# Closing layer 0's tile pools early, and reading the convolution's operands into their room

## The chip, the cores and the metric

The program runs on one core of one Trainium2 chip. Times are device microseconds (us) of one execution. The kernel before takes 4254.93 us, the median of three runs between 4251.25 and 4259.25.

## The reference, cut to what matters

Four layers work on x of shape 4 images x 128 channels x 64 x 64, seen as 128 x 4096 for an image.

```python
x = mamba2d(x)                    # layer 0: projections, a selective scan over 4096 positions, + x
x = x + L1(gn(x))                 # layer 1, see below
t = tokens(x)                     # from here on token-major
t = t + attn2(ln(t)); t = t + ffn(ln(t), L2)     # layer 2: linear attention, 64 experts
t = t + attn3(ln(t)); t = t + ffn(ln(t), L3)     # layer 3
# L1, the "convolution" over a hypergraph, with xf = tokens(gn(x)):
incidence = (dist(xf, xf) < 16)
vert = incidence @ (incidence.T @ (xf @ W_fc.T + b_fc) / deg_e) / deg_v
out = vert + xf
y = gamma * (out - mean(out, over all images)) * rsqrt(var + eps) + beta
return y * sigmoid(y)
```

The mean and variance of layer 1 run over all four images. So y can be made only when the last image's `vert` is done, and the hidden `out` of all images has to wait somewhere. Both `x1` (the output of layer 0) and `hg` (`out`) wait in DRAM, 2 MB an image each.

## The kernel before, in words

**Layers 0 and 1** are written in `layers01` as Python generators. `layer0` yields after each half state of the scan, `layer1(b)` after each piece of work on image b, and the driving loop interleaves layer 1 of image b with layer 0 of image b + 1. Image 3 of layer 1 has no layer 0 beside it and runs alone. Layer 1 of an image first reads the image's x1 in eight chunks `xn` (L457, queue of SyncE, one buffer for each chunk), normalises them on ScalarE (L458), and compares tokens panel by panel on TensorE (L499). At the end it makes `vert` chunk by chunk (L622, 64 matmuls a chunk); VectorE scales it into `rb` (L630), GpSimd adds xn (L631), and `rb` is written to `hg` (L635). When all images are done, five small operations make the scale and shift `bn` (L666 to L671).

**The end of layer 1**, `layer1_end`, takes sixteen units of 128 x 1024 elements. A unit reads `o` from hg (L683, issued on ScalarE's queue) and `x` from x1 (L685, on SyncE's queue), makes silu(o * scale + shift) on ScalarE (L686), adds it to x on GpSimd (L687), turns the sum into tokens by eight transposes on TensorE (L692), and copies the two PSUM tiles into `X`, one by ScalarE and one by VectorE (L694). The pool `l1e` has three buffers for each of o and x.

**Attention of layer 2**, `attn2`, first takes layernorm statistics of 16 blocks of 128 tokens on VectorE (L702), then makes z (L779, L781), turns it on TensorE (L782), and so on. It also reads its own weights (L740, L742) and the first experts' weights (`load`, L1020 and L1023).

**What sets the order.** The operations are written in program order, and a tile framework orders them on each engine by its own priorities; every engine and every DMA queue then runs its own list strictly in order. The tile pools lie in SBUF as a stack, on the left side unless `side="right"` is given; when a pool is closed, a later one takes its room. A pool without `reuse_waits="tile"` that takes room used before waits for all that was done in the pools there; with it, each tile waits for the tiles that it overlaps. DMA completions are counted on eight counters in turn, shared by all queues, and a DMA waits until the one before it on its counter has landed, so about eight are under way at most.

In the kernel before, the pools of layer 0, `l0p` and `l0bc`, stay open until the end of `layers01`, on the left. `X` and then `fe` (one group of experts' weights) are opened after that on the left, then `l1e`.

Of the kernel before, what the change touches and what calls it, by code (L numbers as in the profile page):

```python
# [7 lines left out]
F32 = mybir.dt.float32  # L8
F16 = mybir.dt.float16
FP8 = mybir.dt.float8e4  # L10
AF = mybir.ActivationFunctionType
ALU = mybir.AluOpType
AX = mybir.AxisListType
PSUM = bass.MemoryType.PSUM
DRAM = bass.MemoryType.DRAM

P = 128
B = 4
# [22 lines left out]
class Net:  # L41
# [33 lines left out]
    def layers01(self):  # L75
        nc, tc, a = self.nc, self.tc, self.a
# [9 lines left out]
        LAG = 6 * 2  # L86
        with ExitStack() as ctx:
            wp = ctx.enter_context(tc.tile_pool(name="aw", bufs=1))
            w2 = ctx.enter_context(tc.tile_pool(name="l0p", bufs=2))
            bcp = ctx.enter_context(tc.tile_pool(name="l0bc", bufs=5))  # L90
            tp = ctx.enter_context(tc.tile_pool(name="l1t", bufs=2))
            dp = ctx.enter_context(tc.tile_pool(name="l0d", bufs=3, space=DRAM))
            ip = ctx.enter_context(tc.tile_pool(name="l1i", bufs=1, space=DRAM))
# [2 lines left out]
            ps = ctx.enter_context(tc.tile_pool(name="aps", bufs=4, space=PSUM))  # L96
# [103 lines left out]
            def due(every=False):  # L200
                for w in list(waiting):
                    if every or w[0] <= self.tick:
                        waiting.remove(w)
                        w[1]()
# [445 lines left out]
            for b in range(B):  # L650
                l1 = layer1(b)
                if b < B - 1:
                    done = 0
                    for k in range(states):
                        next(l0, None)
                        self.tick += 1
                        due()
                        while done * states < work * (k + 1):
                            done += next(l1)
                for _ in l1:  # L660
                    self.tick += 1
                    due()
# [7 lines left out]
            nc.vector.tensor_tensor(bn[:, 1:2], bn[:, 2:3], bn[:, 0:1], ALU.mult)  # L670
            nc.vector.tensor_tensor(bn[:, 1:2], gb[:, 1:2], bn[:, 1:2], ALU.subtract)  # L671

    def layer1_end(self):

        nc = self.nc
        with self.tc.tile_pool(name="l1e", bufs=3) as tp, self.tc.tile_pool(
            name="l1eps", bufs=4, space=PSUM
        ) as ps:
            for b in range(B):
                for c in range(4):  # L680
                    sl = slice(c * 1024, (c + 1) * 1024)
                    o = tp.tile([P, 1024], F32, tag="o", name="o")
                    nc.scalar.dma_start(o, self.hg[b][:, sl])  # L683
                    x = tp.tile([P, 1024], F32, tag="x", name="x")
                    nc.sync.dma_start(x, self.x1[b][:, sl])  # L685
                    nc.scalar.activation(o, o, AF.Silu, scale=self.bn[:, 0:1], bias=self.bn[:, 1:2])  # L686
                    nc.gpsimd.tensor_tensor(x, x, o, ALU.add)  # L687
                    for h in range(2):
                        pt = ps.tile([P, 4, P], F32, tag="tr", name="ps_x")
                        for i in range(4):  # L690
                            k = 4 * h + i
                            nc.tensor.transpose(pt[:, i, :], x[:, k * P : (k + 1) * P], self.ident)  # L692
                        k = 8 * c + 4 * h
                        (nc.vector.tensor_copy if h else nc.scalar.copy)(self.X[:, b, k : k + 4, :], pt)  # L694


    def ln_stats(self, sp, b, j0, n, rs=None):
# [577 lines left out]
@with_exitstack  # L1275
def tile_kernel(ctx: ExitStack, tc: tile.TileContext, a, out):
    net = Net(tc, a)
    net.setup(ctx)
    net.layers01()
    xp = ctx.enter_context(tc.tile_pool(name="X", bufs=1))  # L1280
    net.X = xp.tile([P, B, NB, P], F32, tag="X", name="X")
    net.ew = ctx.enter_context(tc.tile_pool(name="fe", bufs=1))
    net.layer1_end()
    net.ahead = net.load(net.ew, "L2_ffn", 0)
    net.attn2()
    net.ffn("L2_ffn")
    net.ahead = net.load(net.ew, "L3_ffn", 0)
    net.attn3()
    net.ffn("L3_ffn", out)
# [48 lines left out]
```

## Time and profile before

| | |
|---|---|
| median of three runs | 4254.93 us |
| the profiled execution | 4245.77 us |
| its span (first to last instruction) | 4244.0 us |
| TensorE, busy | 3520.5 us, 83% of the span |
| VectorE, busy | 3014.7 us, 71% |
| GpSimd, busy | 2463.1 us, 58% |
| ScalarE, busy | 2088.3 us, 49% |
| last write of x1 issued (end of layer 0) | 2848.03 us from the span's start |
| first matmul of layer 1 on image 3 | 2882.45 us |
| last `hg` part computed, bn ready | 3324.5 us |
| last unit of `layer1_end` in X | 3388.8 us |
| first transpose of attention 2 | 3397.4 us |

Times "at" are counted from the start of the span. The busy shares are averages over stages with different limits: an engine at 83% overall can be idle for half of one stage.

### The profile page before, as it was taken

The page shows a single profiled execution, that of the slowest core. Times are in us where ns is not written, and L with a number is a line of the kernel's source. Part 1 is how long each engine was busy: PE and PEld are TensorE (multiplying, and loading weights), DVE is VectorE, ACT ScalarE, POOL GpSimd, SP SyncE. Part 2 cuts the span into 40 slices and gives each one's busy share as a digit, 9 for nine tenths or more (in the row PEclk, how much of TensorE's full clock was granted, in tenths as well). Part 3 has the DMA queues.
Part 4 walks back from the last instruction along what each step waited for, and adds up shares of the span by engine and source line. Part 5 has one row for each costly group of instructions (what it writes and reads, how often), then busy time and mean ns, then how long its engine had stood idle before and what let it go on. Part 6 is the DMA issues. An engine that isn't in the chain of part 4 may idle for free. (4 is left out here: it accounts for less than half of the span.)

```text
span 4244.0 us, 48880 instructions
## 1 busy us (share of the span) xinstructions
PE 3520.5 (83%) x17239; PEld 1963.5 (46%) x17239; DVE 3014.7 (71%) x4819; ACT 2088.3 (49%) x3547; POOL 2463.1 (58%) x1234
## 2 busy tenths in 40 slices
PE   6878858888897788888878888889999589788988
PEld 2333323444533334454334345435664378446844
DVE  5888879987666999866689997665420275746864
ACT  4556654455544545564454555521141287533841
POOL 5999889987786998867788887760000300001300
PEclk8989978999998889999988999999999699898999
DMA  3454534454364444545634454361113400053028
GB/s 105 152 147 146 156 109 134 138 137 138 108 187 139 127 132 137 153 117 146 184 107 135 125 150 126 110 222 70 65 63 112 158 1 1 1 198 124 1 80 299
DMA packets 261991, 523.94 MB, mean 123 GB/s; under 512 B 22346, under 2 KB 24562, under 8 KB 261746
## 3 DMA queue, kind: packets, MB, share of 16 engines
q1 hardware_dynamic: 250450, 501.45, 39.5%
q10 hardware_dynamic: 11296, 19.37, 1.4%
q8 instruction: 136, 2.23, 0.2%
q14 instruction: 109, 0.89, 0.1%
HBM read 443.15 MB, written 77.59 MB: 123 GB/s over the span
## 5 line engine op out<-in xcount | busy, mean ns | idle before, releaser
L286 POOL TENSOR_TENSOR db<-dx,bt 128x1024 f32<-128x1024 f32 x512 | 1203.0, 2353 | 329.3 <-DVE hs L304 214.2
L304 DVE TENSOR_TENSOR_SCAN hs<-hs,carry,db 128x512 f32<-128x512 f32 x812 | 1035.3, 1282 | 177.4 <-ACT hs L298 95.5
L298 ACT ACTIVATE hs<-dl,A 128x512 f32<-128x512 f32 x1024 | 706.5, 692 | 737.3 <-DVE ho L314 684.5
L499 PE MATMUL ps_g<-xn 128*128 128x512 f32 x1152 | 602.8, 654 | 100.7 <-DVE inc L502 74.8
L321 POOL TENSOR_TENSOR ho_s<-ho_s,ho 128x1024 f32<-128x1024 f32 x288 | 677.0, 2351 | 11.6 <-DVE ho L314 10.9
L314 DVE TENSOR_TENSOR ho<-hs,bt 128x1024 f32<-128x1024 f32 x464 | 563.3, 1214 | 1.6
L522 PE MATMUL ps_ed<-xs,inc 128*128 128x258 f16 x4096 | 507.9, 284 | 18.2 <-DVE inc L502 8.1
L522 PEld LDWEIGHTS <-inc 128*128 128x128 fp8e4 x4096 | 414.9, 102 | 131.9 <-issue 60.8
L502 DVE SCALAR_TENSOR_TENSOR inc<-ps_g,hcl,hb 128x512 fp8e4<-128x512 f32 x576 | 420.4, 736 | 35.3 <-PE ps_g L499 19.7
L499 PEld LDWEIGHTS ps_g<-xn 128*128 128x128 f32 x1152 | 216.2, 204 | 416.9 <-DVE inc L502 183.7
L342 PE MATMUL ps_y<-ho,cst 128*128 128x512 f32 x512 | 272.2, 674 | 110.5 <-POOL ho L310 93.1
L622 PE MATMUL ps_v<-inc_v,es 128*128 128x512 fp8e4 x1536 | 342.9, 382 | 19.4 <-DVE rb L630 9.4
L622 PEld LDWEIGHTS <-es 128*128 128x128 f16 x2048 | 202.6, 99 | 288.8 <-issue 63.6
L515 ACT CAST inc<-ps_t 128x512 fp8e4<-128x512 f32 x448 | 232.1, 600 | 96.2 <-PE ps_t L511 96.1
L903 POOL MEMSET G<- 128x128 f32 x2 | 0.4, 204 | 468.2 <-DMA b<-in_L_attn_bv 468.2
L224 PE MATMUL ps_c<-xt,wc 128*128 128x512 f32 x512 | 234.0, 611 | 12.5 <-DVE inc L502 6.8
L342 PEld LDWEIGHTS ps_y<-ho,cst 128*128 128x128 f32 x512 | 104.6, 214 | 269.7 <-POOL ho L310 123.8
L528 ACT COPY ed<-ps_ed 128x129 f32<-128x129 f32 x128 | 34.0, 266 | 377.6 <-PE ps_ed L522 377.6
L529 DVE TENSOR_TENSOR ed<-ps_ed,ed 128x129 f32<-128x129 f32 x128 | 36.6, 286 | 209.7 <-ACT ed L528 206.6
L304 DVE TENSOR_TENSOR_SCAN hs<-hs,db 128x512 f32<-128x512 f32 x116 | 141.3, 1223 | 53.8 <-POOL db L286 42.8
L538 POOL TENSOR_TENSOR ed<-ed,rdeg 128x512 f32<-128x512 f32 x32 | 33.3, 1040 | 250.1 <-DVE rdeg L534 250.1
L224 PEld LDWEIGHTS ps_c<-xt,wc 128*128 128x128 f32 x512 | 99.2, 197 | 139.0 <-issue 116.6
(302 smaller groups left out, 5599.9 us busy)
## 6 DMA issues: line engine op xcount, KB each, us to landing
bt<-bcd SPq DMA_DIRECT2D x512, 512.0 KB
inc<-inc SPq DMA_DIRECT2D x192, 256.0 KB
inc_v<-inc SPq DMA_DIRECT2D x96, 512.0 KB
w<-in_L_ffn_weight SPq DMA_DIRECT2D x32, 1024.0 KB
w2f<-in_L_ffn_weight SPq DMA_DIRECT2D x32, 1024.0 KB
strip<-inc SPq DMA_DIRECT2D x84, 256.0 KB
x<-x ACTq DMA_DIRECT2D x32, 256.0 KB
xn<-x SPq DMA_DIRECT2D x32, 256.0 KB
```

Source lines behind the costliest of these rows:

```text
L224: nc.tensor.matmul(s["ps"][h], wc[:, h, j, :], xt[:, j : j + T], start=j == 0, stop=j == 3)
L286: nc.gpsimd.tensor_tensor(db, s["dx"], bc(s["bt", n][:, 0, :], 2), ALU.mult)
L298: act(nc.scalar.activation(hs[:, k, :], s["dl"][:, k, :], AF.Exp, scale=A[:, k, n : n + 1]))
L304: nc.vector.tensor_tensor_scan(to[:, h, :], hs[:, h, :], db[:, h, :], init, ALU.mult, ALU.add)
L314: nc.vector.tensor_tensor(ho, hs, ct, ALU.mult)
L321: nc.gpsimd.tensor_tensor(s["sum", n // G], s["sum", n // G], ho, ALU.add)
L342: nc.tensor.matmul(s["y"][h], self.ident, t[:, h, :], start=False, stop=n == DS - 1 and k == len(terms) - 1,)
L499: nc.tensor.matmul(pq, xn[v // 4][:, v % 4 * P : (v % 4 + 1) * P], xn[c], start=True, stop=True)
L502: nc.vector.scalar_tensor_tensor(inc[:, v, :], pq, hc[:, v : v + 1], hb, ALU.subtract, ALU.is_gt, saturate=False)
L515: later(1, lambda: act(nc.scalar.copy(inc[:, v, :], pt, saturate=False)))
L522: nc.tensor.matmul(pe[:, : 2 * P + 2], inc[:, v, i * P : (i + 1) * P], xs[:, v, :], start=v == 0, stop=v == NB - 1,)
L622: nc.tensor.matmul(pv, es[:, e, k, :], inc[:, e, :], start=e == 0 and k == 0, stop=e == NB - 1 and k == 1,)
```

## The change

The two pools of layer 0 move to the right side, and are closed as soon as layer 1 of the last image begins. A new function `reload` opens `l1e` in their room, now with ten buffers each for o and x, and writes the reads of the first ten units at that place in the program. The other six units' reads follow one by one, each after a unit of `layer1_end`. All reads of o and x are now on SyncE's queue. In `layer1_end` the additions alternate between GpSimd (even units) and VectorE (odd units). `X` and the PSUM pool of `layer1_end` wait tile by tile.

```diff
@@ layers01
-            w2 = ctx.enter_context(tc.tile_pool(name="l0p", bufs=2))
-            bcp = ctx.enter_context(tc.tile_pool(name="l0bc", bufs=5))
+            only0 = ctx.enter_context(ExitStack())
+            w2 = only0.enter_context(tc.tile_pool(name="l0p", bufs=2, side="right"))
+            bcp = only0.enter_context(tc.tile_pool(name="l0bc", bufs=5, side="right"))
...
                         while done * states < work * (k + 1):
                             done += next(l1)
+                else:
+
+                    only0.close()
+                    self.reload()
                 for _ in l1:
...
+    def reload(self, first=True):
+
+
+        nc = self.nc
+        if first:
+            self.pre = self.tc.tile_pool(name="l1e", bufs=10, side="right", reuse_waits="tile")
+            self.units, self.pool = [], self.pre.__enter__()
+        while len(self.units) < (10 if first else 4 * B):
+            b, c = divmod(len(self.units), 4)
+            sl = slice(c * 1024, (c + 1) * 1024)
+            o = self.pool.tile([P, 1024], F32, tag="o", name="o")
+            nc.sync.dma_start(o, self.hg[b][:, sl])
+            x = self.pool.tile([P, 1024], F32, tag="x", name="x")
+            nc.sync.dma_start(x, self.x1[b][:, sl])
+            self.units.append((o, x))
+            if not first:
+                return
+
     def layer1_end(self):
 
         nc = self.nc
-        with self.tc.tile_pool(name="l1e", bufs=3) as tp, self.tc.tile_pool(
-            name="l1eps", bufs=4, space=PSUM
-        ) as ps:
...
-                    nc.scalar.dma_start(o, self.hg[b][:, sl])
...
-                    nc.sync.dma_start(x, self.x1[b][:, sl])
...
-                    nc.gpsimd.tensor_tensor(x, x, o, ALU.add)
...
+        with self.tc.tile_pool(name="l1eps", bufs=4, space=PSUM, reuse_waits="tile") as ps:
+            for u in range(4 * B):
+                b, c = divmod(u, 4)
+                o, x = self.units[u]
+                nc.scalar.activation(o, o, AF.Silu, scale=self.bn[:, 0:1], bias=self.bn[:, 1:2])
+                (nc.vector if u % 2 else nc.gpsimd).tensor_tensor(x, x, o, ALU.add)
+                for h in range(2):
...
+                self.reload(False)
+        self.pre.__exit__(None, None, None)
@@ tile_kernel
-    xp = ctx.enter_context(tc.tile_pool(name="X", bufs=1))
+    xp = ctx.enter_context(tc.tile_pool(name="X", bufs=1, reuse_waits="tile"))
```

In the built order of instructions, no list differs up to the end of layer 0. TensorE's list is the same but for a few rows in attention 2. The first ten units' reads stand on SyncE's queue between the sixth and the seventh read of xn of image 3, the experts' first w1 stands behind the last write of hg, and on ScalarE's queue five small reads for the experts move from the end of layer 0 to the start of attention 2.

More of the change, by code (lines that the diff above doesn't have):

```diff
@@ L673, in layer1_end @@
     def layer1_end(self):
         nc = self.nc
-        with self.tc.tile_pool(name="l1e", bufs=3) as tp, self.tc.tile_pool(
-            name="l1eps", bufs=4, space=PSUM
-        ) as ps:
[L679 to L682, printed above, removed]
-                    nc.scalar.dma_start(o, self.hg[b][:, sl])
-                    x = tp.tile([P, 1024], F32, tag="x", name="x")
-                    nc.sync.dma_start(x, self.x1[b][:, sl])
[L686 to L694, printed above, removed]
+        with self.tc.tile_pool(name="l1eps", bufs=4, space=PSUM, reuse_waits="tile") as ps:
[5 more added lines that the diff above has]
+                for h in range(2):
+                    pt = ps.tile([P, 4, P], F32, tag="tr", name="ps_x")
+                    for i in range(4):
+                        k = 4 * h + i
+                        nc.tensor.transpose(pt[:, i, :], x[:, k * P : (k + 1) * P], self.ident)
+                    k = 8 * c + 4 * h
+                    (nc.vector.tensor_copy if h else nc.scalar.copy)(self.X[:, b, k : k + 4, :], pt)
+                self.reload(False)
```

## Prediction

> **What bounds the kernel now.** The change touches two places in time, so I read the stages before the lines: busy time of each engine, mean TensorE clock, DMA share and GB/s in stretches that I cut at the landmarks of the table above.
>
> ```profile
> 2860.00:2872.00 12.00, 12.00 (x58) 5.45 (x56) 0.55 (x1) 0.47 (x1) 0.00 (x0) 1.00 0.86 329
> 2872.00:2882.40 10.40, 0.80 (x6) 0.61 (x4) 3.17 (x8) 6.64 (x11) 1.26 (x1) 0.73 0.17 51
> 2900.00:3000.00 100.00, 99.89 (x462) 59.13 (x461) 65.16 (x97) 11.79 (x24) 8.93 (x8) 1.00 0.16 57
> 3222.00:3320.00 98.00, 97.33 (x440) 43.89 (x437) 9.24 (x13) 8.20 (x22) 7.60 (x6) 1.00 0.42 138
> 3325.00:3388.80 63.80, 31.35 (x128) 25.10 (x128) 11.03 (x17) 28.27 (x32) 37.43 (x20) 0.53 0.65 217
> 3388.80:3397.40 8.60, 0.89 (x4) 0.56 (x4) 8.60 (x49) 2.07 (x4) 0.00 (x0) 0.50 0.00 1
> 3450.00:3650.00 200.00, 196.20 (x1361) 162.69 (x1359) 115.43 (x357) 148.99 (x334) 0.00 (x0) 1.00 0.00 1
> ```
>
> The columns after the length are PE, PEld, DVE, ACT, POOL. Image 3's layer 1 (2900 to 3320) and attention 2 (from 3450) are TensorE at 97 to 100%: what delays or advances their start moves the end one for one. Between them lie 72.4 us (3325.0 to 3397.4) in which no engine is over 59%, at first the end of layer 1 (63.8 us), then statistics alone on VectorE (8.6 us). What ends the waits there is in the groups of instructions from 3324 to 3389:
>
> ```profile
> L687 POOL TENSOR_TENSOR x<-x,o 128x1024 f32<-128x1024 f32 x16 | 37.2, 2344 | 27.3 <-ACT o L686 22.6 <-DMA x<-x 3.5 <-PE ps_x L692 1.2
> L692 PE MATMUL ps_x<-cst,x 128*128 128x128 f32 x128 | 31.3, 426 | 37.4 <-POOL x L687 37.4
> L686 ACT ACTIVATE o<-o,bn 128x1024 f32<-128x1024 f32 x16 | 19.6, 1239 | 5.7 <-DMA o<-hg 5.5
> ```
>
> GpSimd's additions carry the stage (37.2 us of 63.8), and they wait 27.3 us in all; the chain that ended last shows for whom:
>
> ```profile
> 3371.18 2.35 POOL x L687
> 3373.58 1.13 PE ps_x L692 x4
> 3374.79 7.55 DMA o<-hg
> 3382.37 1.25 ACT o L686
> 3383.74 2.35 POOL x L687
> ```
>
> With three buffers, the last read of o is issued at 3374.79 and lands 7.55 us later. Reads and ScalarE's order are the second limit.
>
> The start of image 3 is the other place. The timeline there, in order of time:
>
> ```profile
> 2873.28 1.26 POOL L631 TENSOR_TENSOR rb<-rb,xn 128x512 f32<-128x512 f32 x1 [13.46 <-issue]
> 2873.45 1.12 DVE L446 TENSOR_TENSOR nmr<-nmr 128x1 f32<-128x1 f32 x1
> 2874.57 0.32 SPq L635 DMA_DIRECT2D hg<-rb  x1
> 2874.59 0.16 DVE L447 TENSOR_TENSOR nmr<-nmr,mv 128x1 f32<-128x1 f32 x1
> 2874.93 0.43 SPq L457 DMA_DIRECT2D xn<-x  x1
> 2875.99 5.74 ACT L458 ACTIVATE xn<-xn,nmr,rstd 128x512 f32<-128x512 f32 x8 [0.50 <-DVE nmr L452]
> 2882.45 2.08 PE L490 MATMUL ps_hb<-sq,ones 128*128 128x512 f32 x2 [7.26 <-ACT sq L463]
> ```
>
> The last read of xn is issued at 2874.93; ScalarE takes the eight chunks in 5.74 us without waiting for it, and TensorE starts at 2882.45.
>
> **What the Trainium skill says.** SBUF — State Buffer, section Who interferes with whom: a tensor_tensor of VectorE with both inputs in SBUF and a GpSimd operation that reads SBUF exclude each other, and the later one waits to the end. The trace agrees: a 128x1 product of L446 took 1.12 us and ended just as GpSimd's addition did, its like at L447 0.16 us. DMA: Bandwidth & Descriptors, section Queues, rings and completion order: SyncE's reads share one row of rings, consumed in order. Nothing in the trace of before contradicts that; no stretch shows it alone. TensorE: Matmul & The Clock Gate, Part 1: a busy window of about 3.4 us lifts the clock from half to full. The trace has 0.53 in the stage, where TensorE is half idle, and 1.00 in the convolution.
>
> **Step 1, the reads come early.** Twenty reads of 512 KB (10.5 MB) move to the start of image 3. Twelve more (6.3 MB) stay in the stage. Ahead of the reads on SyncE are the reads for the last vert of image 2, so TensorE's work up to 2872.4 keeps its time. Behind them are the reads of xn[6] and xn[7]. The queue's order: three units, the hg write of 2859.85, nine more reads, the hg write of 2874.57, five more, then xn[6] and xn[7]. Nine reads from 2859.9 are 4.7 MB; at the 329 GB/s of the first row above that is 14.3 us, so they have landed about when the second hg write goes. Five more are 2.6 MB, 8.0 us at 329 GB/s, 7 us at the 375 that 3 us stretches between 2856 and 2868 show. From 2875.5 they end at 2883, the two xn (0.5 MB, 1.5 us) at 2884.5, and a completion takes about 1.5 us: xn[7] is there at 2886 where ScalarE took it at 2881.0 before (the last 0.72 of 5.74 us). **Cost +5 us**, between 3 (375 GB/s and short completions) and 12 (250 GB/s). It goes one for one to the end: TensorE has no idle time in the row 2900 to 3000 to take it up. The DMA engines are at 16% there, so nothing later in image 3 meets the reads.
>
> **Step 2, the stage itself.** It keeps its 16 silus, 32 copies and 128 transposes; 8 of 16 additions move. By engine, with no waits: ScalarE 16 x (1.17 + 0.48), from three silus in 3.50 us and from a copy at 3334.49 followed by a silu at 3334.97, = 26.4 us. TensorE at half clock 128 x 0.22 (1.57 us of weight loads for eight, and the hand-over) = 28 us, about half if the clock rises. Additions: GpSimd 8 x 2.344 = 18.8; VectorE has no row with both inputs in SBUF at this size; nearest is ho<-hs,bt with one input in PSUM, 1.21 us, and I take 1.2, so 9.6. As they exclude each other they add: 28.4 us. VectorE has its 16 copies (11.1), about 45 statistics at 0.20 (9) and the additions: 30 us. So four chains of 26 to 30 us run through queues that are in order, and none is hidden by another. A pair of units costs 3.55 us of additions if VectorE is always ready; where it must first finish copies that wait for transposes of the unit before, I count another 1.5 us every second pair, 4.3 us a pair. First addition at 3326.3, the eighth of GpSimd at 3326.3 + 7 x 4.3 = 3356.4, ends 3358.8; VectorE's last to 3360.0; eight transposes to 3361.8; the last copy to 3362.5.
>
> **Step 3, the reads that remain.** The first experts' w1 (1 MB) moves from 2854 to 3322.5 and is there by 3327. Each of the six units waits for the buffers of the unit ten before it, the last for unit 5, about 3342. 6.3 MB from 3329 at 260 GB/s (the stage shows 217 with waits, single rows up to 370) end at 3353; unit 15 is needed at 3355. Close, but hidden; at 220 GB/s they end at 3358 and cost 3.
>
> **Step 4, into attention 2.** VectorE's statistics of the first 16 blocks now run inside the stage. What is left behind the last copy is the scaling of attention's weights (5 operations, 1.6 us with the transpose) and z: first transpose at about **3365.4**, against 3397.4, **-32 us**. The weights' read stands behind all units and w2 (1 MB) and lands at 3353 to 3358, hidden by the last units; at 220 GB/s at 3363, which costs 1. ScalarE gets four small reads ahead of z (4 x 0.5 us, beside VectorE's 2.1) and one behind. Two more table loads of 1.28 us stand in its list in attention 2, where ScalarE and TensorE take turns at first: **+1**, bounds 0 and 2.6.
>
> **At nothing**: the ob memsets and w2, needed 300 us later; l0p and l0bc at other addresses, where the lists of layers 0 and 1 are the same.
>
> Sum against the profiled execution: -32 + 5 + 1 = -26, 4245.8 to 4219.8 us; the median of the runs lies 9.2 higher, so **4229 us**. Differences under 0.2% (8.5 us) can't be told from no change here.
>
> **Rivals.** *A larger gain* (0.15): TensorE warms up, the clash of additions costs less because ScalarE is the slowest anyway, pairs at 3.5 us: first transpose at 3360, xn late by 3: -37 + 3 = -34, 4221 us and below. For it: 1.00 clock wherever TensorE is busy. Against: in-order copies on VectorE. *A smaller gain* (0.17): additions alternate badly (5 us a pair, first transpose at 3370.5), reads at 220 GB/s, xn late by 9: -27 + 12 = -15, 4240 us. Against: 329 GB/s in the row above. *Not what it says* (0.03): the stage goes on waiting for reads and handing over as before, and only the statistics move into it: -8.6 + 5 + 1 = -3, 4252 us. Against it: the ten units stand in the queue 440 us ahead. *Slower* (0.05): the reads ahead of xn hold image 3. This decides at a delay of 31 us, so xn[7] at 2912; 11 MB from 2851 then take 61 us, 180 GB/s. At 150 GB/s they take 73 us, the delay is 43 us, and the time 4267 us. Against: 240 and 329 GB/s in that very stretch. The forecast itself (-21 to -32) has 0.60.
>
> **Range.** 4217 (about -38, the larger gain's half) to 4241 (the smaller gain's end) holds 8 in 10. Faster 0.92 (the forecast and the two gains), same 0.04, slower 0.04: the slower rival's edge reaches into the same.
>
> **What would show it.** After: last xn issued about 2877.5, first matmul of image 3 at 2886 to 2889; no DMA behind silu in the stage; additions of VectorE that take up to 3.5 us where they meet GpSimd's; first transpose of attention 2 minus bn ready at 41 us instead of 73. Wrong would make me: an x addition waiting for reads through the stage, or a TensorE gap at 2872 of over 20 us.

## The result and the profile after

The changed kernel took 4234.08 us, the median of four runs (4230.31 to 4234.85), beside 4255.5 us for the kernel before: ratio 0.9948, 95% interval 0.9931 to 0.9965. Two later comparisons gave 0.9932 (0.9919 to 0.9945) and 0.9931 (0.9916 to 0.9946). It is faster by 21 to 31 us; the forecast was 26 us and 4229 us.

I cut the profile after at the landmarks of the one before. The stretches are the last reads ahead of image 3, its start, and the stage from the batch statistics to attention 2. The columns after the length are the busy times of PE, PEld, DVE, ACT and POOL, then the granted clock, the DMA share and GB/s.

```profile
2867.00:2883.00 16.00, 16.00 (x74) 7.24 (x73) 1.45 (x2) 1.87 (x2) 1.26 (x1) 1.00 0.88 288
2883.00:2892.00 9.00, 1.09 (x7) 0.77 (x5) 3.18 (x8) 4.59 (x7) 1.26 (x1) 0.78 1.00 369
3343.00:3382.50 39.50, 23.69 (x131) 20.05 (x131) 32.47 (x70) 29.55 (x37) 22.02 (x10) 0.75 0.61 219
```

The last row answers to two rows of before, 63.8 and 8.6 us. The work is in 39.5 us now, and VectorE and ScalarE, busy 0.82 and 0.75 of it, come closest to full. The groups of instructions in that stretch show who waits for whom:

```profile
L709 PE MATMUL ps_x<-cst,x 128*128 128x128 f32 x128 | 23.0, 349 | 19.1 <-POOL x L704 15.8 <-DVE x L704 3.2
L704 POOL TENSOR_TENSOR x<-x,o 128x1024 f32<-128x1024 f32 x8 | 21.5, 2694 | 14.4 <-ACT o L703 11.5 <-PE ps_x L709 2.9
L703 ACT ACTIVATE o<-o,bn 128x1024 f32<-128x1024 f32 x16 | 19.2, 1238 | 0.0
L704 DVE TENSOR_TENSOR x<-x,o 128x1024 f32<-128x1024 f32 x8 | 12.6, 1574 | 3.4 <-ACT o L703 3.4
```

No addition and no silu waits for a DMA; before, 5.5 us of silus and 3.5 us of additions did. The additions take 2694 ns on GpSimd and 1574 on VectorE, where alone they take 2.34 (in the kernel before) and 1.22 (in a run below): they get in each other's way. A piece of the chain that ended last:

```profile
3350.93 2.41 POOL x L704
3353.34 0.04 issue
3353.39 0.67 PE ps_x L709 x4
3354.06 0.02 issue
3354.08 0.58 ACT X L711
3354.66 1.15 ACT o L703
3355.81 0.07 issue
3355.88 2.36 POOL x L704
```

Where the chain before had a read of 7.55 us between two additions, it now has a transposition, a copy and a silu: ScalarE's list holds a silu behind a copy, and the copy behind the transposes of the unit before. At the start of image 3 the timeline has the price:

```profile
2884.57 1.26 POOL L632 TENSOR_TENSOR rb<-rb,xn 128x512 f32<-128x512 f32 x1 [13.46 <-issue]
2888.78 1.34 SPq L458 DMA_DIRECT2D xn<-x  x2
2898.35 1.52 ACT L459 ACTIVATE xn<-xn,nmr,rstd 128x512 f32<-128x512 f32 x2 [6.73 <-DMA xn<-x]
2900.58 2.08 PE L491 MATMUL ps_hb<-sq,ones 128*128 128x512 f32 x2 [14.10 <-ACT sq L464]
```

From image 2's last addition of rb to image 3's first matmul it took 2882.45 - 2873.28 = 9.2 us before and takes 2900.58 - 2884.57 = 16.0 us now; ScalarE waits 6.73 us for the last two reads of xn.

Already ahead of the first moved read, at 2855.74, the two profiles are 11.3 us apart (a write of hg at 2842.06 before and at 2853.40 after, and the same at rb, 2873.28 and 2884.57), in code whose lists of instructions are the same. This had to be explained first, since it is as large as the terms to be judged.

### The profile page after: what moved, and what is told of

Its sections match the earlier page's. It is cut to its first block, busy times and chain, and to the rows that moved or that the text cites. A ratio compares the mean times of both kernels' runs of the same rounds, so it can differ in the third digit from the quotient of the medians.

```text
span 4232.8 us, 48856 instructions
## 1 busy us (share of the span) xinstructions
PE 3533.5 (83%) x17239; PEld 1967.7 (46%) x17239; DVE 3031.5 (72%) x4827; ACT 2089.5 (49%) x3549; POOL 2446.4 (58%) x1226
```

## Experiments

The table has the landmarks of every profile: the start of the last addition of rb in image 2; from there to image 3's first matmul (gap); from that to the last operation of bn (image 3); to the first transpose of attention 2 (stage); to the end of the span (rest). There is one profile for each row. The times are medians of the runs, the ratios against the kernel before on the same chip.

| kernel | rb | gap | image 3 | stage | rest | time, us | ratio (95%) |
|---|---|---|---|---|---|---|---|
| before, first profile | 2873.3 | 9.2 | 441.9 | 73.1 | 846.6 | 4255.5 | |
| before, again | 2886.7 | 9.2 | 441.9 | 70.2 | 856.3 | 4253.6 | 0.9997 (0.9987-1.0008) |
| changed, first profile | 2884.6 | 16.0 | 441.8 | 40.2 | 850.3 | 4234.1 | 0.9948 (0.9931-0.9965) |
| changed, again | 2885.3 | 15.5 | 439.7 | 39.7 | 850.1 | 4230.1 | 0.9932 (0.9919-0.9945) |
| changed, third | 2874.0 | 16.3 | 441.6 | 40.2 | 850.2 | 4227.9 | 0.9931 (0.9916-0.9946) |
| right side only | 2879.9 | 9.2 | 442.0 | 77.0 | 864.5 | 4267.4 | 1.0023 (1.0013-1.0032) |
| xn first | 2873.8 | 9.2 | 441.8 | 40.2 | 853.8 | 4229.8 | 0.9931 (0.9918-0.9944) |
| xn first, again | 2888.8 | 9.2 | 441.8 | 40.2 | 853.6 | 4230.5 | 0.9932 (0.9912-0.9952) |
| additions on GpSimd | 2880.5 | 15.1 | 440.0 | 52.6 | 850.9 | 4244.3 | 0.9967 (0.9955-0.9978) |
| three buffers | 2884.9 | 9.2 | 441.8 | 66.5 | 857.5 | 4247.9 | 0.9980 (0.9970-0.9990) |
| additions on VectorE | 2880.0 | 16.1 | 441.7 | 38.8 | 853.6 | 4232.3 | 0.9942 (0.9922-0.9962) |
| additions on TensorE | 2880.6 | 15.9 | 441.9 | 61.7 | 851.2 | 4246.9 | 0.9982 (0.9971-0.9994) |
| VectorE and xn first | 2872.2 | 9.2 | 441.9 | 38.8 | 853.7 | 4215.8 | 0.9896 (0.9881-0.9912) |
| the same, 4 copies moved | 2877.6 | 9.2 | 441.8 | 37.0 | 855.6 | 4222.9 | 0.9913 (0.9898-0.9927) |

### The 11 us ahead of the change: executions, or addresses?

The first theory is that executions differ there; the second that the new addresses of layer 0's pools cost it. The kernel before and the changed kernel were profiled again, the latter twice, and one kernel has the new side and nothing else.

> The kernel before, unchanged, for a second profile. The two profiles at hand differ by 11.3 us already at the end of layer 0 (2848.0 before, 2859.3 after), in code whose instruction lists are the same. If executions simply differ there (first theory), this profile ends layer 0 anywhere from 2846 to 2862, and a second profile nearer the median of 4255 than 4245.8 ends it near 2857. If the new addresses of the pools l0p and l0bc cost it (second theory), layer 0 ends here at 2846 to 2850 again. From the end of layer 0 to the batch statistics being ready 476 us, and from there to the first transpose of attention 2 72 to 74 us, under both.

> The changed kernel again. Ratio 0.993 to 0.9965 as before. Both theories: 482 to 484 us from the end of layer 0 to the batch statistics, about 40 us from there to the first transpose of attention 2. First theory: the end of layer 0 lies anywhere from 2846 to 2862; second: 2857 to 2861 again.

> The changed kernel a third time, beside the next one on the same chip, since the two medians so far (4230.1 and 4229.8 us) leave open whether 6.6 us at the start of image 3 reach the end. Ratio 0.992 to 0.9945, gap from the last addition of rb to the first matmul of image 3 15 to 17 us.

```diff
-            w2 = ctx.enter_context(tc.tile_pool(name="l0p", bufs=2))
-            bcp = ctx.enter_context(tc.tile_pool(name="l0bc", bufs=5))
+            w2 = ctx.enter_context(tc.tile_pool(name="l0p", bufs=2, side="right"))
+            bcp = ctx.enter_context(tc.tile_pool(name="l0bc", bufs=5, side="right"))
```

> The kernel before with only the two pools of layer 0 on the right side of SBUF: other addresses, nothing closed early, no read moved. First theory (executions differ): ratio 0.9995 to 1.0005, 4253 to 4257 us, and the end of layer 0 as scattered as that of the kernel before. Second theory (addresses): layer 0 ends at 2857 to 2861 and the time is 8 to 12 us up, ratio 1.002 to 1.003. The rest as in the kernel before: 476 us to the batch statistics, 73 us to the first transpose.

The kernel before, profiled again, reached the same addition of rb 13.4 us later than the first time; the changed kernel, a third time, 10.6 us earlier than the first. So executions of one kernel differ by as much as the 11.3 us, and nothing points to the change: the twelve profiles in the table with layer 0's pools on the right reach rb at 2880.2 us in the mean, the two with them on the left at 2880.0. One place where the two profiles of the kernel before part is seen on SyncE's queue, at two of layer 0's reads of its input, and in the stretch between them. The first profile:

```profile
558.45 0.34 SPq L217 DMA_DIRECT2D xt<-in_x  x1
830.28 0.35 SPq L217 DMA_DIRECT2D xt<-in_x  x1
```

```profile
600.00:800.00 200.00, 160.20 (x527) 79.78 (x526) 191.35 (x247) 105.06 (x149) 183.00 (x84) 0.88 0.46 129
```

and the second:

```profile
558.99 0.35 SPq L217 DMA_DIRECT2D xt<-in_x  x1
838.72 0.35 SPq L217 DMA_DIRECT2D xt<-in_x  x1
```

```profile
600.00:800.00 200.00, 165.00 (x499) 80.33 (x497) 184.80 (x239) 101.22 (x143) 175.08 (x80) 0.84 0.48 126
```

Up to the first of these reads the two are 0.5 us apart, and at the second 8.4 us. Between them the granted clock is 0.84 where it was 0.88. What moved it isn't shown.

The new side alone was slower by 11 us (0.13 to 0.32%), as the second theory said, but not where it said: at rb it lies between the two profiles of the kernel before. Two other parts are longer, the stage (77.0 against 70.2 and 73.1) and the rest (864.5 against 846.6 and 856.3). The queue of SyncE and the first silu's wait show a reason for the stage. In this kernel:

```profile
3330.39 1.27 SPq L685 DMA_DIRECT2D x<-x  x3
3331.71 0.78 SPq L1020 DMA_DIRECT2D w<-in_L_ffn_weight  x1
3332.53 0.83 SPq L1023 DMA_DIRECT2D w2f<-in_L_ffn_weight  x1
3336.22 1.28 ACT L686 ACT_TABLE_LOAD   x1 [5.82 <-DMA o<-hg]
```

and in the kernel before, second profile:

```profile
2866.42 1.27 SPq L685 DMA_DIRECT2D x<-x  x3
2867.73 0.81 SPq L1020 DMA_DIRECT2D w<-in_L_ffn_weight  x1
```

With layer 0's room on the right and the pools that follow on the left, the first three units' reads and the first experts' two weights lose the room in which they were read some 460 us ahead. They go out together as the stage begins, and ScalarE waits 5.82 us for the first o, for which it did not wait in the kernel before. So both theories missed, the first in the time, the second in the place: moving the pools without closing them early costs some 4 to 7 us in the stage. How much of the longer rest belongs to the edit stays open, since the kernel before itself shows 846.6 and 856.3 there. The first theory is enough for the 11.3 us.

### The start of image 3: order or traffic?

```diff
@@ layer1, after the eight reads of xn
+                if b == B - 1:
+                    only0.close()
+                    self.reload()
@@ the driving loop
-                else:
-                    only0.close()
-                    self.reload()
```

> The changed kernel with the first ten units' reads written after image 3's eight reads of xn, which the planner turns into this order on SyncE: each of the last two xn reads follows at once the write of hg ahead of it, so that xn[7] has fifteen of the twenty reads ahead of it and not twenty, xn[6] twelve less than before. If the 6.8 us that image 3 loses at its start are the wait of xn[7] behind five reads issued after the last write of hg, the gap from the last rb to the first matmul goes from 16.9 us back to 10 to 12 and the time falls by 5 to 7 us, ratio to the kernel before 0.993. If they come from the traffic alone, whatever the order (nine reads still under way when that write goes), the gap stays at 14 to 17 us and the time falls by 3 us at most. The end of the layer and attention 2 as in the changed kernel: 40 us.

The timeline of this kernel at the start of image 3, and the stretch around it:

```profile
2875.48 0.43 SPq L458 DMA_DIRECT2D xn<-x  x1
2876.54 5.74 ACT L459 ACTIVATE xn<-xn,nmr,rstd 128x512 f32<-128x512 f32 x8 [0.50 <-DVE nmr L453]
```

```profile
2872.00:2881.00 9.00, 1.35 (x8) 0.87 (x6) 3.17 (x8) 4.72 (x8) 1.26 (x1) 0.80 1.01 378
```

The DMA engines moved 378 GB/s here, no less than the 369 in the changed kernel, and yet ScalarE takes the eight chunks in 5.74 us as in the kernel before. So it is the order and not the traffic: with five reads fewer ahead of the last xn, and fourteen fewer ahead of the one before it, the whole 6.8 us are gone. This agrees with what the Trainium skill says in DMA: Bandwidth & Descriptors, Queues, rings and completion order: SyncE's transfers share one row of rings, and each DMA engine consumes a ring's descriptors in order.

The time, however, did not follow: 4229.84 us beside 4230.10, where 5 to 7 us less were expected. Both kernels were run again.

> The kernel with xn's last reads ahead, again. Its first profile had the gap back at 9.2 us, 6.6 us less, but its median was that of the changed kernel. If the delay goes one for one to the end: 4 to 8 us below the changed kernel over both pairs of runs, ratio to the kernel before 0.991 to 0.9925. If attention 2 gives it back (that profile's 853.8 us from the first transpose to the end, against 850.2): within 3 us of the changed kernel, and 853 us or more there again.

Again the same time, within what can be told. Over both pairs of comparisons, twelve runs of this kernel have a mean of 4229.5 us and eleven of the changed kernel 4229.3, a difference of 0.2 with a standard error of about 2.5 (from the scatter of the runs). Gap, image 3 and stage are as they should be in the profiles, so the saving reaches attention 2 whole; but the rest is 853.8 and 853.6 us where the changed kernel has 850.3, 850.1 and 850.2, so 3.5 us come back there. What is left of the 6.8, 3.3 us, can't be told from nothing with that error.

Apart from the place of two reads on SyncE's queue the two kernels have the same lists on every engine. Attention 2 is not where they part: both reach the first `h` of layer 2's experts 389.7 us after its first transpose (389.4 in one profile). They part in what follows, from that `h` to the last `eo` of the sixteen groups of experts. The rows of this stretch, in order for the changed kernel (first profile), xn first (first profile), and the kernel before (first and second profile):

```profile
3772.22:3848.07 75.85, 64.85 (x734) 31.44 (x726) 11.84 (x20) 11.31 (x19) 2.67 (x12) 0.84 1.00 364
3754.73:3834.26 79.53, 68.46 (x734) 32.86 (x726) 11.84 (x20) 11.31 (x20) 2.67 (x12) 0.79 0.96 347
3779.62:3857.72 78.10, 66.18 (x734) 32.16 (x726) 11.85 (x20) 11.31 (x20) 2.61 (x12) 0.83 0.97 354
3792.75:3877.86 85.11, 74.10 (x734) 35.67 (x726) 11.84 (x20) 11.31 (x19) 2.61 (x12) 0.72 0.90 325
```

TensorE has the same 734 instructions in each, and the length goes with its busy time and the granted clock: over all fourteen profiles it runs from 75.8 us at a clock of 0.84 to 87.7 us at 0.69, and what is left beside TensorE's busy time is 11.0 to 12.2 us. What sets the clock there isn't shown. Two profiles of the kernel before part by 7.0 us in it, so the 3.5 us can't be put down to the edit. The pair with all additions on VectorE, below, speaks against it: there the same edit takes 7.0 us off the gap and the rest is 853.6 and 853.7. So "one for one" held through image 3, and in that pair of profiles to the end; for this pair the runs leave it open.

### The stage: depth, split, and what bounds it now

First the changed kernel without one of the two parts: all additions on GpSimd again, and three buffers again. Both keep the other parts of the change.

```diff
-                (nc.vector if u % 2 else nc.gpsimd).tensor_tensor(x, x, o, ALU.add)
+                nc.gpsimd.tensor_tensor(x, x, o, ALU.add)
```

> The changed kernel with all sixteen additions on GpSimd, as in the kernel before: reads early and ten buffers deep, but no split. Theory A (the additions are the chain of the stage, and the split shortened it): sixteen additions of 2.34 us, one behind the other, are 37.5 us from bn + 2 us on, and VectorE's last transposes, copies and z follow in 6 us: first transpose of attention 2 at 45 to 47 us after the batch statistics, against 40 with the split, so 5 to 7 us slower than the changed kernel, ratio to the kernel before 0.9945 to 0.9955. Theory B (the early reads are all of the gain, and the split gives nothing because the two engines exclude each other): 40 to 41 us and the ratio of the changed kernel, 0.993.

```diff
-            self.pre = self.tc.tile_pool(name="l1e", bufs=10, side="right", reuse_waits="tile")
+            self.pre = self.tc.tile_pool(name="l1e", bufs=3, side="right", reuse_waits="tile")
...
-        while len(self.units) < (10 if first else 4 * B):
+        while len(self.units) < (3 if first else 4 * B):
```

> The changed kernel with three buffers for x and o, where it has ten: the split and the early closing stay, seven units are no longer read ahead. The three units' reads leave xn free, so the gap at the start of image 3 is 9 to 10 us again. Theory A (reads ahead carry most of the 32 us): a unit's buffer comes free after its transposes, its next read takes 7.5 us to land, and silu, addition and transposes 5 to 6 us: 13 us for three units, sixteen units in 58 to 66 us, first transpose 60 to 68 us after the batch statistics, so the kernel is 13 to 22 us slower than the changed one, ratio to the kernel before 0.996 to 0.999. Theory B (the split and the statistics carry it): 45 us or less, ratio 0.993 or lower.

The additions in the groups of instructions of the first kernel,

```profile
L704 POOL TENSOR_TENSOR x<-x,o 128x1024 f32<-128x1024 f32 x16 | 37.4, 2369 | 10.5 <-ACT o L703 10.5
```

and of the second:

```profile
L704 POOL TENSOR_TENSOR x<-x,o 128x1024 f32<-128x1024 f32 x8 | 20.9, 2614 | 38.1 <-ACT o L703 26.9 <-DVE lnnm L727 6.9 <-DMA x<-x 4.3
L704 DVE TENSOR_TENSOR x<-x,o 128x1024 f32<-128x1024 f32 x8 | 12.8, 1600 | 3.9 <-ACT o L703 2.9 <-DMA x<-x 1.0
```

On GpSimd alone the stage takes 52.6 us, more than the 45 to 47 of theory A: to the 37.4 us of additions come 10.5 us of waits for silus, which I had put at nothing. With three buffers it takes 66.5 us, as theory A said, and additions wait for reads once more. From the mean of the kernel before (71.6), the kernel with depth but no split gains 19 us, the one with the split but no depth 5, and both together 31.6. Part of each is neither: VectorE's statistics. From the last copy into X to the first transpose it takes 8.6 us in both profiles of the kernel before and 2.3 to 2.5 us in these two kernels and the changed one, since most statistics now run before that copy. Up to the last copy (its end counted from bn ready) the times are 64.4 and 61.5 us before, 49.9 with depth alone, 63.9 with the split alone, and 37.2 to 37.7 with both. So depth alone brings 13 us, the split alone nothing, both 25.4, and the statistics 6.2 in any case: with reads on the path the split has nothing to shorten, and with one engine for all additions the depth has 37.4 us in its way. Which part of the change moves the statistics was not tested apart.

Then two ways to be rid of the clash of additions: all on VectorE, or none.

```diff
-                (nc.vector if u % 2 else nc.gpsimd).tensor_tensor(x, x, o, ALU.add)
+                nc.vector.tensor_tensor(x, x, o, ALU.add)
```

> The changed kernel with all sixteen additions on VectorE and none on GpSimd, so that no two of them can exclude each other. Theory A (lock): each addition takes 1.21 us, not up to 2.34; VectorE has 16 x 1.21 + 16 x 0.68 for copies + 64 statistics at 0.2 + small operations = 46 us less those statistics that the last blocks leave for later, so 38 to 43 us from the batch statistics to the first transpose of attention 2: same as the changed kernel within 3 us, with VectorE as the full engine, over 0.9 busy. Theory B (GpSimd's slow additions are the bound, not the lock): 33 to 36 us.

```profile
L704 DVE TENSOR_TENSOR x<-x,o 128x1024 f32<-128x1024 f32 x16 | 19.3, 1218 | 1.8 <-ACT o L703 1.8
```

```profile
3338.00:3376.60 38.60, 18.76 (x131) 15.67 (x131) 36.77 (x82) 28.93 (x37) 0.56 (x2) 0.85 0.62 226
```

Sixteen additions take 1218 ns each, with nothing beside them, and VectorE does all sixteen in 19.3 us where the two engines needed 34.1 for the same. Yet the stage is only 1.4 us shorter, because VectorE is now busy for 36.77 of 38.60 us: theory A. The last copy ends 7 us sooner, 30.4 us after bn, but 8.2 us pass from there to the first transpose, with VectorE busy on the statistics that it had no room for. The clash was worth no more than what VectorE had to spare.

```diff
-                (nc.vector if u % 2 else nc.gpsimd).tensor_tensor(x, x, o, ALU.add)
...
-                        nc.tensor.transpose(pt[:, i, :], x[:, k * P : (k + 1) * P], self.ident)
+                        for t in (x, o):
+                            nc.tensor.matmul(
+                                pt[:, i, :], t[:, k * P : (k + 1) * P], self.ident, start=t is x, stop=t is o
+                            )
```

> The changed kernel without additions on VectorE or GpSimd: TensorE multiplies both x and o by the identity and sums them in PSUM, 256 multiplications where there were 128 transposes. Theory A (additions and their lock are the stage's chain): ScalarE's list is left as the longest, 16 x (1.24 + 0.58) + 1.3 = 30.4 us, and TensorE has 256 x 0.11 to 0.22: 28 us with the clock up, 56 us with it down. With TensorE busy all along the clock should rise: first transpose of attention 2 at 33 to 37 us, 3 to 7 us less than the changed kernel, ratio to the kernel before 0.9915 to 0.9925. Theory B (the clock stays half and TensorE becomes the bound): 50 us or more, 10 us slower than the changed kernel. The gap at the start of image 3 stays 16 us in all these kernels but the one with three buffers.

```profile
L709 PE MATMUL ps_x<-cst,o 128*128 128x128 f32 x256 | 50.6, 282 | 4.9 <-ACT o L703 4.9
L709 PE MATMUL ps_x<-cst,x 128*128 128x128 f32 x248 | 49.0, 280 | 0.0
```

```profile
3338.50:3345.00 6.50, 4.58 (x22) 4.58 (x23) 0.09 (x1) 6.49 (x7) 0.00 (x0) 0.51 0.91 308
3345.00:3400.00 55.00, 54.41 (x488) 54.17 (x486) 41.46 (x196) 30.85 (x41) 0.56 (x2) 1.00 0.37 121
```

Both theories missed. The clock did rise, from 0.51 over the first 6.5 us to 1.00 in the rest, and TensorE became the bound all the same, at 54.41 of 55 us. An f32 product by the identity is two instructions with two weight loads here (x256 for the 128 products of o; of the 256 for x the trace has 248), where the 128 transposes are 128. So a unit has 32 instructions where it had eight, an estimated 3.6 us (55 us by 488, times 32), and the eight transposes of the changed kernel took 1.06 to 1.09 us at their fastest in its timeline. The stage lost 21.5 us.

### Both mended at once

The two savings together, and then four of VectorE's copies given to ScalarE:

> Both at once: xn's last reads ahead, and all sixteen additions on VectorE. Gap at the start of image 3 9.2 us (-6.6), 38.6 us from the batch statistics to the first transpose of attention 2 (-1.3), so 8 us below the changed kernel if both reach the end, ratio to the kernel before 0.991 to 0.992; 0.9925 or more if they do not.

```diff
-                    (nc.vector.tensor_copy if h else nc.scalar.copy)(self.X[:, b, k : k + 4, :], pt)
+                    (nc.vector.tensor_copy if h and u % 4 < 3 else nc.scalar.copy)(self.X[:, b, k : k + 4, :], pt)
```

> The kernel ahead with four of VectorE's sixteen copies on ScalarE. VectorE was busy 36.8 of 38.6 us there, ScalarE 28.9: four copies are 2.8 us off VectorE and 2.3 us on ScalarE, 34.0 and 31.2. If VectorE is the bound: first transpose 36 to 37 us after the batch statistics, 2 us less. If the order of ScalarE's list is (a copy that waits for transposes holds the silu behind it): 39 us or more. In the time 2 us can't be told from nothing.

With all additions on VectorE and xn first the kernel takes 4215.79 us, ratio 0.9896 (0.9881 to 0.9912): better than the changed kernel's 0.9931 (0.9916 to 0.9946) on the same chip, better than the 0.991 to 0.992 expected, and the fastest of all that were run. Gap and stage are as foreseen, 9.2 and 38.8 us. By the profiles it should gain 6.8 + 1.4 - 3.5 = 4.7 us on the changed kernel; the medians say 12.1, with a standard error of about 2 from the scatter of the runs. Where the other 7 lie, ahead of image 3 or after it, isn't settled.

With four copies moved the stage is 37.0 us, 1.8 us shorter, as a full VectorE demands:

```profile
3328.60:3365.50 36.90, 18.88 (x131) 15.69 (x131) 34.81 (x78) 30.80 (x41) 0.56 (x2) 0.87 0.64 236
```

Its rest is 1.9 us longer and its median 7 us higher; it shows the bound of the stage and is no gain in time.

## Why the prediction was right

**The sum.** Stage by stage, with the means of two profiles of before and three of after: gap +6.8, image 3 -0.8, stage -31.6, rest -1.3, in all -26.9 us, beside -26 forecast. The medians gave -21.4, -26.3 and -31.5 in three comparisons. That -26.9 comes so near is in part luck: the rest of the two profiles of before differs by 9.7 us, so its mean is not known to 1.3. That the first profiles before and after differ by 11.2 us only comes from stretches that the change doesn't touch: 11.3 us ahead of image 3, and a rest of 846.6 us in the first profile of before, 4.9 under the mean of the two.

**Step 1, the reads come early: +5, measured +6.3 to +7.1.** The order on SyncE's queue, the delay of the last xn and the bounds held. Mis-sized was what is still under way at the second write of hg: I let the six reads ahead of the first write be gone by then, and the nine between the writes move at 329 GB/s and be done. But three of the six went out only at 2866.83 to 2867.67, 4 us before the first write (2871.14), since the queue waited for a transfer of x to land, as its waits show (total, times, longest):

```profile
SPq L691 <- DMA x<-x: 8.5, 1, 8.5
```

So twelve reads (6.3 MB) were issued from 2866.83 on, and the 288 GB/s of the first row above are 4.6 MB in its 16 us. The last two xn were issued 4.2 and 5.2 us after rb, where 4.2 was forecast, and ScalarE took the last one 14.5 us after rb instead of 12.7: 1.8 us later than forecast, the difference between 5 and 6.8. Through image 3 the delay went on one for one. That it goes so to the end, the pair with all additions on VectorE shows in its profiles; with the split additions it could not be shown.

**Step 2, the stage itself.** Pairs of units start every (3372.67 - 3344.37) / 7 = 4.04 us in the mean, forecast 4.3; the last copy ends 37.7 us after bn, forecast 38. The reason given, that additions on GpSimd and VectorE exclude each other, is what the durations show: VectorE's take 1.22 us alone and up to 2.34 beside GpSimd's (up to 3.5 was forecast), GpSimd's up to 3.34. Some addition runs for 27.3 of the 33.0 us from the first to the last, forecast 28.4. The 5.7 us between are as long as the 6 us that I counted for VectorE's copies, but that is luck as to their place: what ended 11.5 of GpSimd's 14.4 us of waits was a silu, which stands on ScalarE behind a copy that waits for transposes. How close the chains lie, as the forecast said, the runs bear out: taking the clash away shortened the stage by 1.4 us, for VectorE's list was next. That TensorE could take over the additions and gain, which I expected later, was wrong.

**Step 3, the reads that remain, hidden.** No addition, silu or transpose of the stage waits for a DMA in the changed kernel.

**Step 4, into attention 2: -32, measured -31.6** from bn to the first transpose, 39.7 to 40.2 us where 40.9 were forecast. The statistics run inside the stage, as said, and are 6.2 of the 31.6 us. The **+1** for table loads can't be read from the rest, most of whose scatter is in the experts, but it can be from attention 2: the first `zf` of layer 2's experts starts 258.5 and 259.6 us after the first transpose before and 260.9 to 261.0 after, 1.3 to 2.5 us later, with thirteen table loads up to there instead of eleven. With all additions on VectorE there are eleven again, and it starts at 258.6. What the forecast doesn't have is the part from there to the first `h`: 128.7 us at a granted clock of 0.79 in the changed kernel, 123.7 and 125.3 at 0.85 and 0.86 before. In the rest this is made up by the experts, at 0.84. Whether it belongs to the change isn't shown.

**At nothing.** Other addresses of l0p and l0bc cost layer 0 nothing that shows. That the same edit without the early closing costs 4 to 7 us in the stage does not bear on the forecast, since here the pools are closed early.

**The rivals.** The slower one, image 3 held for 31 us or more by the reads ahead of xn, had the right place, but the gap grew by 6.8 us only: reads moved at 288 to 369 GB/s, far above the 180 at which it would decide. "Not what it says" falls with the depth: additions and silus no longer wait for reads. The smaller gain asked for pairs at 5 us, the larger one for pairs at 3.5; it was 4.04.

## What to carry to other kernels

Count a prefetch's cost at the reads that it is put ahead of, not at its own: here 512 KB reads put ahead of two 256 KB reads on one queue cost 6.8 us, and issuing the needed reads first took that away at the same DMA rate. Where a read and a slow operation alternate on the path, a second engine for the operation is worth nothing until the reads are deep enough: alone the depth brought 13 us up to the last copy, the split none, both 25. And before a single profile's difference is put down to a change, compare stretches whose instructions the change doesn't touch, and their granted clock: here two profiles of one kernel differed by 13.4 us in one such stretch and 9.7 in another, about half the gain.

## What the runs showed that I had not expected

- Two executions of one kernel differ by 13.4 us at the same instruction 2.87 ms in; 7.9 us of it arise in one stretch of some 275 us, in whose middle 200 us the granted clock is 0.88 in one and 0.84 in the other.
- In the experts of layer 2, 734 instructions of TensorE that are the same in every kernel took 75.8 to 87.7 us over the fourteen profiles, as the granted clock there was 0.84 to 0.69.
- Adding two f32 tiles on TensorE by products with the identity costs an estimated 3.6 us for 128 x 1024 at a granted clock of 1.00, over three times the 1.06 to 1.09 us of the transposes that it replaces.
- VectorE's addition of 128 x 1024 from SBUF takes 1.22 us alone, about half of GpSimd's 2.34; sharing the sixteen additions between both keeps them busy for 34.1 us in all, and VectorE alone for 19.3.
